# An attention-pooling recommender on one core: the order of VectorE's product and of the head's second layer

## The chip, the cores and the metric

The kernel runs on one core of a Trainium2 chip. The metric is the device time of one execution in microseconds (us); of several runs the median is taken. The profile is one more execution, taken with the hardware profiler.

## The reference

A batch of 16384 users has a history of 200 items each. Every embedding row has D = 64 numbers; the item table has some 100000 rows.

```python
it = i_emb[item]                       # [16384, 64]
h = i_emb[hist]                        # [200, 16384, 64]
itb = jnp.broadcast_to(it[None], h.shape)
feat = jnp.concatenate([h, itb, h - itb, h * itb], axis=-1)
a = dice(feat @ au_W1 + au_b1, au_alpha, axis=1)
w = a @ au_W2 + au_b2
cur = jnp.sum(w * h, axis=0)
z = jnp.concatenate([u, it, c, cur], axis=-1)
z = dice(z @ W1 + b1, alpha1, axis=0)
z = dice(z @ W2 + b2, alpha2, axis=0)
return z @ W3 + b3
```

`dice` normalises over the batch axis, takes a sigmoid p of the result, and gives `x * (p + alpha * (1 - p))`. So each of the 200 history layers needs the mean and variance of its whole batch before its weights can be computed.

## The kernel before, in words

The batch is cut into ND = 8 chunks of 2048 rows (128 partitions by TD = 16 rows). One **step** handles one chunk of one history layer; 200 layers by 8 chunks make 1600 steps. The first 168 layers run in a hardware loop (`tc.For_i`, seven passes) whose body is written out for 24 layers (192 steps); the remaining 32 layers and the head stand behind it. Inside each stretch the order of the instructions on every engine is the program's own (`manual_schedule`): an engine works through its queue in that order and waits where data aren't there.

At the start a table is built in DRAM that holds, beside each item row, that row already multiplied by its part of `au_W1`; a gather then fetches both halves, 512 bytes, at once. What depends on the item alone is computed once and kept in DRAM (`xi`).

`step(k)` works on several chunks at different ages:

- `fetch(k)`: POOL issues sixteen gathers (L202), each of 128 rows, into one of twelve landing buffers `land`; SP loads a piece of `xi` into `xit`.
- for chunk k-10, ScalarE: the sigmoid (L448) and the mixing with alpha (L451), into the PSUM tile `pg`.
- for chunk k-1: `turn` (L377), four transposes by VectorE from `land` into `hx`; ScalarE copies the transposed h into the PSUM tile `ph` (L454).
- for chunk k-2: `hidden`, VectorE adds `px` and the table's half (L390) and takes the batch statistics (L392).
- for chunk k-1: ScalarE puts `xit` into `px` (L458); `product` has VectorE multiply h by the item (L384, from `ph` and `itT` into `hx`), and TensorE adds the product of that with `blk_m` onto `px` (the L240 rows with `hx,blk_m`). The next step's `hidden` reads this `px`.
- once in a layer: `moments`, from the statistics to the scale and shift that the sigmoid uses.
- for chunk k-10: `weigh`, VectorE alone: a product (L398), a transpose (L400), a sum (L402), small copies and additions into the PSUM tile `ph` (L406, L409), the product with h (L414) and the addition to `cur` (L415).

After the last fetch ten more steps drain the pipeline, with the head's first layer between them. The head's second layer goes over the eight chunks: the activation `dice` (ScalarE L563, VectorE L564 and L565) of 64 of the hidden units, and once in four chunks (J = 4) of the rest of them; eight matmuls of 128 by 80 (L240, `w2a` and `w2b`) into one of four PSUM tiles in turn; ScalarE's copy out with the bias (L595); VectorE's statistics (L525). A third activation and the output layer (L604) end the kernel.

Of the kernel before, what the change touches and what calls it, by code (L numbers as in the profile page):

```python
# [10 lines left out]
AF = mybir.ActivationFunctionType  # L11
# [17 lines left out]
def din_kernel(  # L29
# [24 lines left out]
    nc = tc.nc  # L54
# [3 lines left out]
    ND = NT // TD  # L58
    V = i_emb.shape[0]
    A = au_W1.shape[1]  # L60
    Z1, Z2, ZO = W1.shape[1], W2.shape[1], W3.shape[1]
# [9 lines left out]
    def quarter(e, g, n=S):  # L71

        return slice((2 * e + g) * S, (2 * e + g) * S + n)
# [24 lines left out]
    for e in range(2):  # L98
        rows = au_W1.rearrange("(g d) a -> d g a", d=D)[e * S : (e + 1) * S]
        for g in range(2):  # L100
            r = quarter(e, g)
            nc.sync.dma_start(au_w[r], rows)
            for q, (a0, n) in enumerate(parts):
                c, a = quarter(q, g, n), slice(a0, a0 + n)
# [3 lines left out]
    for g in range(2):  # L108
        for q, (a0, n) in enumerate(parts):
            r, a = quarter(q, g, n), slice(a0, a0 + n)  # L110
# [18 lines left out]
    px, pz = (psum.tile([P, CD], F32, name=n) for n in ("px", "pz"))  # L129
    ph = psum.tile([P, CD], F32, name="ph")  # L130
    pg = psum.tile([P, CD], F32, name="pg")
# [9 lines left out]
    J = P // (2 * ZB)  # L141
    w1a = const.tile([P, 4, P], F32, name="w1a")
    w1b = const.tile([P, 4, P + 2 * ZB * (J - 1)], F32, name="w1b")
    w2a = const.tile([P, 2 * Z2], F32, name="w2a")
    w2b = const.tile([P, J, 2 * Z2], F32, name="w2b")
    w3 = const.tile([2 * Z2, (2 * ND - 1) * 2 * ZO], F32, name="w3")

    za, zb, z2 = (
        [const.tile([n, 1], F32, name=f"{m}{i}") for i in ("b", "al", "1al")]
        for m, n in (("za", P), ("zb", P), ("z2", 2 * Z2))  # L150
    )
# [83 lines left out]
    def layer(dst, pairs, n=CH, onto=False):  # L235

        for i in range(2):
            cols = slice(i * CH, i * CH + n)
            for j, (lhsT, rhs) in enumerate(pairs):
                nc.tensor.matmul(  # L240
                    dst[:, cols], lhsT, rhs[:, cols],
                    start=(j == 0 and not onto), stop=(j == len(pairs) - 1),
                    skip_group_check=onto,
                )
# [90 lines left out]
    with ExitStack() as main:  # L335
# [24 lines left out]
        def by_row(t):  # L360
            return t.rearrange("p (n d) -> p n d", d=D)

        def x_of(k):
            return land[k % LAND][:, :, D:]
# [16 lines left out]
        def product(k):  # L381

            hm = hx[k % 2][:, 0]
            nc.vector.tensor_mul(hm, ph, itT[:, k % ND])  # L384
            layer(px, [(blk_m, hm)], onto=True)
# [7 lines left out]
                    stats[l % 2][:, 2 * c + i, :], x_of(k)[:, ts(i, TD // 2)]  # L393
                )

        def weigh(k):

            nc.vector.tensor_mul(by_row(pg), by_row(pg), x_of(k))  # L398
            yT = hx[k % 2][:, 0]
            nc.vector.transpose(yT, pg)  # L400
            r = small.tile([P, 2, TD], F32, tag="r", name="r")
            nc.vector.tensor_reduce(  # L402
                r, yT.rearrange("p (i n u) -> p i n u", i=2, u=S), mybir.AxisListType.X, ALU.add
            )
            r1 = small.tile([D, 2, TD], F32, tag="r1", name="r1")
            nc.vector.tensor_copy(r1, r[D:])  # L406
            w = ph[:, :TD]
            for i in range(2):
                nc.vector.scalar_tensor_tensor(  # L409
                    w[ts(i, D)], r[:D, i], au_bias2[:D], r1[:, i], ALU.add, ALU.add  # L410
                )
            c = k % ND
            rows = land[k % LAND][:, :, :D]
            nc.vector.tensor_mul(by_row(pg), rows, w.unsqueeze(2).to_broadcast([P, TD, D]))  # L414
            nc.vector.tensor_add(cur[:, ts(c, TD)], by_row(pg), cur[:, ts(c, TD)])  # L415
# [22 lines left out]
        def step(k, last=None):  # L438


            def has(j):
                return last is None or j <= last

            if has(k):
                fetch(k)
            if has(k - 10):
                i = (k - 10) // ND % 2
                nc.scalar.activation(  # L448
                    by_row(pg), x_of(k - 10), AF.Sigmoid, bias=shifts[i], scale=rstds[i]
                )  # L450
                nc.scalar.activation(pg, pg, AF.Identity, bias=au_al, scale=au_1al)  # L451
            if has(k - 1):
                turn(k - 1)
                nc.scalar.copy(ph, hx[(k - 1) % 2][:, 0])  # L454
            if has(k - 2):
                hidden(k - 2)
            if has(k - 1):
                nc.scalar.copy(px, xit[(k - 1) % XI])  # L458
                product(k - 1)
            if has(k - 2) and (k - 2) % ND == ND - 1:  # L460
                moments((k - 2) // ND)
            if has(k - 10):
                weigh(k - 10)

        def fetch_ids(k, l0, n):
            l, c = divmod(k, ND)
# [40 lines left out]
        def home(i):  # L507
            t = land[(K + i // 2) % LAND].rearrange("p (s n) d -> p s (n d)", s=2)
            return t[:, i % 2]
# [6 lines left out]
        def rest_of(c):  # L516
            return home(homes[ND + c // J])
# [5 lines left out]
        def row_sums(i, n, m, t):  # L523
            for h in range(2):
                nc.vector.bn_stats(zstats[i][:, 2 * m + h, :], t[:n, ts(h, CH)])  # L525
# [18 lines left out]
        def row_factors(i, unit, n):  # L544

            mean_mat = mean_of[unit]
            mv = small.tile([P, 2], F32, tag=f"zmv{i}", name="zmv")[:n]
            nc.vector.bn_aggr(mv, zstats[i].rearrange("p c s -> p (c s)"))
            mean = ph[:n, i * 8 : i * 8 + 1]
            nc.tensor.matmul(mean, mean_mat, mv[:, 0:1], start=True, stop=True)  # L550
            dev = small.tile([P, 1], F32, tag=f"zdev{i}", name="zdev")[:n]
            nc.vector.tensor_sub(dev, mv[:, 0:1], mean)
            nc.vector.scalar_tensor_tensor(dev, dev, dev, mv[:, 1:2], ALU.mult, ALU.add)
            var = ph[:n, i * 8 + 4 : i * 8 + 5]
            nc.tensor.matmul(var, mean_mat, dev, start=True, stop=True)  # L555
            rstd = small.tile([P, 1], F32, tag=f"zrstd{i}", name="zrstd")[:n]
            shift = small.tile([P, 1], F32, tag=f"zshift{i}", name="zshift")[:n]
            return scale_and_shift(mean, var, n, rstd, shift)
# [8 lines left out]
        with tc.manual_schedule():  # L567
            work = base_of_layer1()
            for k in range(K):
                fetch_ids(k, L - rest_l, rest_l)  # L570
                step(k, last=K - 1)
                next(work, None)
            load_base(0, 1)
            for k in range(K, K + 10):
                step(k, last=K - 1)
                if k < K + 4:
                    load_base(*((2, 3), (ND, ND + 1), (4, 5), (6, 7))[k - K])
                c = k - K - 2
                if c >= 1:
                    keep1(c - 1)  # L580
                if c >= 0:
                    layer1(c)
            keep1(ND - 1)

            spare = [home(i) for i in range(18, 24)]
            fa, fb = row_factors(0, ZA, P), row_factors(1, ZB, P)
            for c in range(ND):
                if c % J == 0:
                    dice(rest_of(c), rest_of(c), spare[4 + c // J], fb, zb)
                a = spare[c % 4]  # L590
                dice(a, z_of(c), a, fa, za)
                po = (px, pz, pg, ph)[c % 4]
                layer(po[: 2 * Z2], [(w2a, a), (w2b[:, c % J], rest_of(c))])
                t = home(10 + c)[: 2 * Z2]
                nc.scalar.activation(t, po[: 2 * Z2], AF.Identity, bias=z2[0])  # L595
                row_sums(2, 2 * Z2, c, t)
            f2 = row_factors(2, Z2, 2 * Z2)
            n = ND * 2 * ZO
            for c in range(ND):
                a = spare[c % 4]  # L600
                dice(a, home(10 + c)[: 2 * Z2], a, f2, z2)
                at = (ND - 1 - c) * 2 * ZO
                for i in range(2):
                    nc.tensor.matmul(  # L604
                        px[:n, ts(i, CH)], w3[:, at : at + n], a[: 2 * Z2, ts(i, CH)],
                        start=(c == 0), stop=(c == ND - 1),
                    )

            rT, res = spare[4][:S], spare[5][:S]
            nc.vector.transpose(rT, px[:S])  # L610
            rT = rT.rearrange("t (i n c g o) -> t i g c n o", i=2, n=TD, c=ND, g=2)
            for i in range(2):
                for g in range(2):
                    nc.vector.tensor_add(
                        res[:, ts(2 * i + g, NT * ZO)].rearrange("t (c n o) -> t c n o", c=ND, n=TD),
                        rT[:, i, g],
                        bias3.unsqueeze(1).unsqueeze(1).to_broadcast([S, ND, TD, ZO]),
                    )
            nc.sync.dma_start(
                out.rearrange("(q t n) o -> t q (n o)", t=S, n=NT),  # L620
                res.rearrange("t (q m) -> t q m", q=4),
            )
# [30 lines left out]
```

## Time and profile before

| what | value |
|---|---|
| time, median of 3 runs | 36757.6 us (36756.6 to 36763.1) |
| profiled execution, its own time | 32783.1 us |
| its span, first to last instruction | 32780.9 us |
| POOL: busy, and the gathers L202 in it | 24515.6 us; 25600 of 943 ns |
| VectorE (DVE): busy | 25567.4 us |
| ScalarE (ACT), TensorE (PE): busy | 7755.2 us, 6366.6 us |
| drain and first layer of the head (32515 to 32650) | 135 us |
| second layer of the head (32650 to 32740) | 90 us |
| output layer (32740 to the end) | 41 us |

The profiled execution is shorter than the runs shown; durations below are from it. In a line of a group the columns are: line and engine, operation, output and inputs, shapes, count, then busy time in us, the mean of one in ns, and the engine's idle time just before with what ended it. "Issue" is idle time in which the engine waited for nothing that the profile shows. In a timeline they are: start and length in us, engine, line, operation, and in brackets the idle time before and what released it.

### The profile page before, as it was taken

The page shows a single profiled execution, that of the slowest core. Times are in us where ns is not written, and L with a number is a line of the kernel's source. Part 1 is how long each engine was busy: PE and PEld are TensorE (multiplying, and loading weights), DVE is VectorE, ACT ScalarE, POOL GpSimd, SP SyncE. Part 2 cuts the span into 40 slices and gives each one's busy share as a digit, 9 for nine tenths or more (in the row PEclk, how much of TensorE's full clock was granted, in tenths as well). Part 3 has the DMA queues.
Part 4 walks back from the last instruction along what each step waited for, and adds up shares of the span by engine and source line. Part 5 has one row for each costly group of instructions (what it writes and reads, how often), then busy time and mean ns, then how long its engine had stood idle before and what let it go on. Part 6 is the DMA issues. An engine that isn't in the chain of part 4 may idle for free. (4 is left out here: it accounts for less than half of the span.)

```text
span 32780.9 us, 100656 instructions
## 1 busy us (share of the span) xinstructions
PE 6366.6 (19%) x7006; PEld 2038.0 (6%) x7006; DVE 25567.4 (78%) x28797; ACT 7755.2 (24%) x7105; POOL 24515.6 (75%) x25991
## 2 busy tenths in 40 slices
PE   3111111111111111111111111111111112221112
PEld 0000000000000000000000000000000000000000
DVE  7777777777777777777777777777777777777777
ACT  1222222222222222222222222222222222222222
POOL 7777777777777777777777777777777777777775
PEclk5555555555555555555555555555555555555555
DMA  5222222222222222222222222222222223332222
GB/s 157 80 79 79 79 79 79 79 79 79 79 80 80 79 78 79 79 79 80 79 79 79 79 79 78 79 79 80 78 79 79 79 79 85 88 90 81 79 79 60
DMA packets 1214773, 2667.86 MB, mean 81 GB/s; under 512 B 551244, under 2 KB 577388, under 8 KB 1207916
## 3 DMA queue, kind: packets, MB, share of 16 engines
q0 software_dynamic: 831488, 1691.97, 19.6%
q1 hardware_dynamic: 372012, 906.09, 9.1%
q10 hardware_dynamic: 10560, 63.79, 0.5%
q14 instruction: 692, 5.67, 0.1%
q8 instruction: 21, 0.34, 0.0%
HBM read 2590.90 MB, written 69.16 MB: 81 GB/s over the span
## 5 line engine op out<-in xcount | busy, mean ns | idle before, releaser
L202 POOL DMA_INDIRECT land<-table,idx x25600 | 24152.2, 943 | 7872.6 <-issue 7703.8
L377 DVE STREAM_TRANSPOSE hx<-land 64x1024 f32<-64x1024 f32 x6404 | 7938.2, 1240 | 6360.3 <-DMA land<-table,idx 6218.5
L240 PE MATMUL px<-hx,blk_m 128*128 128x512 f32 x6408 | 5927.6, 1080 | 26007.0 <-DVE hx L384 25941.1
L448 ACT ACTIVATE pg<-land,sh,rs 128x1024 f32<-128x1024 f32 x1610 | 1943.8, 1207 | 12980.0 <-DVE cur L415 11593.3
L454 ACT COPY ph<-hx 128x1024 f32<-128x1024 f32 x1601 | 1627.6, 1017 | 10365.2 <-DVE hx L377 10362.2
L240 PEld LDWEIGHTS px<-hx,blk_m 128*128 128x128 f32 x6408 | 1880.1, 324 | 30022.8 <-issue 29846.4
L392 DVE BATCH_NORM_STATS2 st<-land 128x6 f32<-128x512 f32 x3204 | 2060.9, 685 | 55.0
L400 DVE STREAM_TRANSPOSE hx<-pg 128x1024 f32<-128x1024 f32 x1610 | 2011.7, 1250 | 55.2
L414 DVE TENSOR_TENSOR pg<-land,ph 128x1024 f32<-128x1024 f32 x1610 | 1977.8, 1228 | 55.0
L415 DVE TENSOR_TENSOR cur<-pg,cur 128x1024 f32<-128x1024 f32 x1610 | 1970.5, 1224 | 55.6
L402 DVE TENSOR_REDUCE r<-hx 128x32 f32<-128x1024 f32 x1610 | 1964.0, 1220 | 55.3
L390 DVE TENSOR_TENSOR land<-px,hx 128x1024 f32<-128x1024 f32 x1602 | 1961.6, 1224 | 49.5
L398 DVE TENSOR_TENSOR pg<-pg,land 128x1024 f32<-128x1024 f32 x1610 | 1968.8, 1223 | 2.7 <-ACT pg L451 2.5
L384 DVE TENSOR_TENSOR hx<-ph,itT 128x1024 f32<-128x1024 f32 x1601 | 1932.0, 1207 | 0.0
L451 ACT ACTIVATE pg<-pg,au_al,au_1al 128x1024 f32<-128x1024 f32 x1610 | 1895.0, 1177 | 54.3
L458 ACT COPY px<-xit 128x1024 f32<-128x1024 f32 x1601 | 1627.2, 1016 | 383.3 <-DVE land L390 381.1
L409 DVE SCALAR_TENSOR_TENSOR ph<-r,au_bias,r 64x16 f32<-64x16 f32 x3220 | 771.3, 240 | 114.8
L406 DVE COPY r<-r 64x32 f32<-64x32 f32 x1610 | 337.2, 209 | 55.0
L448 ACT ACT_TABLE_LOAD x209 | 268.1, 1283 | 452.6 <-DVE w1a L177 314.6
L249 ACT ACT_TABLE_LOAD x203 | 260.4, 1283 | 6.7 <-PE ph L555 3.2
L249 ACT ACTIVATE std<-var,eps 128x1 f32<-128x1 f32 x201 | 59.2, 295 | 475.2 <-DVE var L435 475.2
L425 DVE COPY other<-mv 32x2 f32<-32x2 f32 x804 | 155.6, 194 | 15.1
(122 smaller groups left out, 1885.8 us busy)
## 6 DMA issues: line engine op xcount, KB each, us to landing
xit<-xi SPq DMA_DIRECT2D x1601, 512.0 KB
land<-table,idx POOLq DMA_INDIRECT x25600
table<-tab ACTq DMA_DIRECT2D x48, 1024.0 KB
tab<-in_L_rec_i_emb SPq DMA_DIRECT2D x48, 512.0 KB
zt<-ucT SPq DMA_DIRECT2D x32, 512.0 KB
idx<-in_r_hist SPq DMA_DIRECT2D x200, 64.0 KB
ucT<-t ACTq DMA_DIRECT2D x16, 512.0 KB
zbase<-zt SPq DMA_DIRECT2D x10, 512.0 KB
```

The costliest lines, as they stand in the source:

```text
L202: nc.gpsimd.indirect_dma_start(out=dst[:, n, :], out_offset=None, in_=rows, in_offset=bass.IndirectOffsetOnAxis(ap=ids[:, n : n + 1], axis=0),
L240: nc.tensor.matmul(dst[:, cols], lhsT, rhs[:, cols], start=(j == 0 and not onto), stop=(j == len(pairs) - 1), skip_group_check=onto,)
L377: nc.vector.transpose(dst.rearrange("p s (n t) -> p n s t", t=S), rows[ts(i, D), :, :, e])
L384: nc.vector.tensor_mul(hm, ph, itT[:, k % ND])
L390: nc.vector.tensor_add(x_of(k), by_row(px), by_row(hx[k % 2][:, 1]))
L392: nc.vector.bn_stats(stats[l % 2][:, 2 * c + i, :], x_of(k)[:, ts(i, TD // 2)])
L398: nc.vector.tensor_mul(by_row(pg), by_row(pg), x_of(k))
L400: nc.vector.transpose(yT, pg)
L402: nc.vector.tensor_reduce(r, yT.rearrange("p (i n u) -> p i n u", i=2, u=S), mybir.AxisListType.X, ALU.add)
L414: nc.vector.tensor_mul(by_row(pg), rows, w.unsqueeze(2).to_broadcast([P, TD, D]))
L415: nc.vector.tensor_add(cur[:, ts(c, TD)], by_row(pg), cur[:, ts(c, TD)])
L448: nc.scalar.activation(by_row(pg), x_of(k - 10), AF.Sigmoid, bias=shifts[i], scale=rstds[i])
```

## The change

Two edits of order. `weigh` is cut in two: its first half, now `weights` (L398, L400, L402), runs on VectorE ahead of `product` (L384 and its matmuls), and its second half stays behind product and moments. In the head's second layer the activation and the matmuls of chunk c (`activated`) are written ahead of the copy out and the statistics of chunk c-2 (`keep2`), in place of each chunk's copy out directly behind its matmuls. No instruction is added or removed.

```diff
-        def weigh(k):
+        def weights(k):
 
             nc.vector.tensor_mul(by_row(pg), by_row(pg), x_of(k))
             yT = hx[k % 2][:, 0]
@@
                 r, yT.rearrange("p (i n u) -> p i n u", i=2, u=S), mybir.AxisListType.X, ALU.add
             )
+            return r
+
+        def weigh(k, r):
+
             r1 = small.tile([D, 2, TD], F32, tag="r1", name="r1")
             nc.vector.tensor_copy(r1, r[D:])
@@
             if has(k - 1):
                 nc.scalar.copy(px, xit[(k - 1) % XI])
+            if has(k - 10):
+                r = weights(k - 10)
+            if has(k - 1):
                 product(k - 1)
             if has(k - 2) and (k - 2) % ND == ND - 1:
                 moments((k - 2) // ND)
             if has(k - 10):
-                weigh(k - 10)
+                weigh(k - 10, r)
@@
-            for c in range(ND):
+            def activated(c):
                 if c % J == 0:
                     dice(rest_of(c), rest_of(c), spare[4 + c // J], fb, zb)
                 a = spare[c % 4]
                 dice(a, z_of(c), a, fa, za)
-                po = (px, pz, pg, ph)[c % 4]
-                layer(po[: 2 * Z2], [(w2a, a), (w2b[:, c % J], rest_of(c))])
+                layer(
+                    (px, pz, pg, ph)[c % 4][: 2 * Z2], [(w2a, a), (w2b[:, c % J], rest_of(c))]
+                )
+
+            def keep2(c):
                 t = home(10 + c)[: 2 * Z2]
-                nc.scalar.activation(t, po[: 2 * Z2], AF.Identity, bias=z2[0])
+                nc.scalar.activation(
+                    t, (px, pz, pg, ph)[c % 4][: 2 * Z2], AF.Identity, bias=z2[0]
+                )
                 row_sums(2, 2 * Z2, c, t)
+
+            for c in range(ND + 2):
+                if c < ND:
+                    activated(c)
+                if c >= 2:
+                    keep2(c - 2)
```

## The prediction

> **What bounds the kernel now.** I read the page first, then the list of waits, then the timeline of one step in mid-run, and at last the timeline of the head. Of the page, these lines carry most (busy time and share of the span; then a group's count, its busy time, the mean in ns, and the idle time before it with what ended it):
>
> ```profile
> PE 6366.6 (19%) x7006; PEld 2038.0 (6%) x7006; DVE 25567.4 (78%) x28797; ACT 7755.2 (24%) x7105; POOL 24515.6 (75%) x25991
> ...
> L202 POOL DMA_INDIRECT land<-table,idx x25600 | 24152.2, 943 | 7872.6 <-issue 7703.8
> L377 DVE STREAM_TRANSPOSE hx<-land 64x1024 f32<-64x1024 f32 x6404 | 7938.2, 1240 | 6360.3 <-DMA land<-table,idx 6218.5
> ```
>
> VectorE is the busier engine, and yet it isn't the bound. POOL's idle time before the gathers is almost all "issue": it waited for nothing, and 24152 + 7873 = 32025 us is 98% of the span. VectorE's one large wait is for the gathers to land: 6218 us, 3.9 us in each of the 1600 steps. The timeline shows the same in one step (start, length, engine, line):
>
> ```profile
> 16025.28 1.22 DVE L398 TENSOR_TENSOR pg<-pg,land 128x1024 f32<-128x1024 f32 x1
> 16025.29 0.94 POOL L202 DMA_INDIRECT land<-table,idx  x1 [0.31 <-issue]
> ...
> 16025.51 3.75 PE L240 MATMUL px<-hx,blk_m 128*128 128x512 f32 x4 [16.17 <-DVE hx L384]
> ...
> 16036.68 5.00 DVE L377 STREAM_TRANSPOSE hx<-land 64x1024 f32<-64x1024 f32 x4 [4.36 <-DMA land<-table,idx]
> ```
>
> A gather starts every 1.248 us (0.943 and 0.305 of issue), whatever VectorE is doing; sixteen make 19.97 us, and the step is 20.0 us. VectorE is done with its step at 16032.3 and then waits 4.36 us. So **POOL's gathers set the 32 ms of the loop**; what moves inside VectorE's step has 4.3 us of room.
>
> The head, the last 0.27 ms, has no gathers. In its second layer each chunk runs alone:
>
> ```profile
> 32661.12 1.11 ACT L595 ACTIVATE land<-px,z2b 80x1024 f32<-80x1024 f32 x1 [8.98 <-PE px L240]
> 32662.13 1.23 ACT L563 ACTIVATE land<-land,zshift,zrstd 128x1024 f32<-128x1024 f32 x1
> 32662.26 1.28 DVE L525 BATCH_NORM_STATS2 zst<-land 80x6 f32<-80x512 f32 x2 [7.17 <-ACT land L595]
> 32663.46 0.79 DVE L564 TENSOR_SCALAR land<-land,za1al,zaal 128x1024 f32<-128x1024 f32 x1
> 32664.29 1.22 DVE L565 TENSOR_TENSOR land<-land,land 128x1024 f32<-128x1024 f32 x1
> ...
> 32665.57 1.99 PE L240 MATMUL pz<-land,w2a 128*80 128x512 f32 x2 [4.49 <-DVE land L565]
> ...
> 32671.45 1.11 ACT L595 ACTIVATE land<-pz,z2b 80x1024 f32<-80x1024 f32 x1 [8.09 <-PE pz L240]
> ```
>
> ScalarE evacuates chunk c (L595), only then takes the sigmoid of c+1 (L563), VectorE finishes the activation, and only then TensorE starts. One chunk costs 10.33 us (32661.12 to 32671.45), of which TensorE works 5.9.
>
> **What the Trainium skill says.** (1) "SBUF — State Buffer", Who interferes with whom: a VectorE instruction with at most one SBUF input, outside the two-port modes, does not contend with GpSimd, while an fp32 copy inside SBUF can take the shared ports and hold up the writing of descriptors. The moved product L384 reads ph (PSUM) and itT, one SBUF input; the gather's 943 ns shows no trace of any of VectorE's instructions. (2) "PSUM — Partial Sum Buffer", Engine vs sequencer instructions: the queues of ScalarE and VectorE are strict FIFO. The trace agrees: L563 of the next chunk starts 1.01 us after L595 each time, never ahead of it. (3) "TensorE: Matmul & The Clock Gate", What's actually happening: the array runs at half clock until it has been busy for some 3.4 us. The trace agrees in this stage: matmuls start 0.85 us apart, after about 4.5 us of work 0.43 apart. But it does not always hold: the output layer L604 (80 rows by 32 columns) keeps 0.85 us for all of its 27.5 us.
>
> **The product moved (L384 behind L398, L400, L402).** Nothing is added or taken away in a step, no DMA among it; SP's and POOL's queues issue what they did, in the same order and past nothing new.
> - VectorE's own sum. From start to next start I read L392 to L384 0.59 us, L384 to L398 1.12, L398 to L400 1.26, L400 to L402 1.28, L402 to L406 1.25. In the new order the reduction is followed by an instruction that doesn't need its result, and so is the product: 0.59 + 1.26 + 1.28 + 1.12 + 1.12 instead of 0.59 + 1.12 + 1.26 + 1.28 + 1.25, that is 0.13 us less. It lies under the 4.3 us of waiting for the gather: worth 0.
> - What L398 now waits for: L451 of ScalarE, which ended at 16014.9 for a VectorE step that starts at 16016.7. Met.
> - What is later: TensorE's product, by 1.26 + 1.28 + 1.12 = 3.7 us. It would run from 16029.2 to 16033; who waits for it is L390 of the next step, at about 16041.7. 8.7 us of room are left. If the landing wait were gone, 4.4 us would be left.
> - The moments stay behind the product and move with it; their sqrt sits on ScalarE behind the copies, and the next sigmoid waits for L415 in either order. Worth 0.
> - The drain after the last gather (some 135 us) has one step where cover is short: the last product ends at about 32534.7, and L390, which started at 32533.8, waits some 0.9 us. Cost 1 us, once.
> - Loop ends (six between the seven passes): at the one I read, TensorE would end near 8173.1, and POOL's last gather at 8175.2 still comes last. Worth 0.
>
> **The second layer two chunks ahead.** L563 of c+1 and c+2 go ahead of L595 of c, so TensorE has two chunks queued. From the end of chunk c: 1.01 (L595) + 1.16 (L563) + 0.1 + 0.83 (L564) + 1.23 (L565) give the next operand after 4.4 us, against two chunks of 8 x 0.43 = 3.44 us, 6.9 us, that TensorE still has. TensorE becomes the bound: five matmuls at 0.85 and 59 at 0.43 make 29.6 us. VectorE's sum is as long: 8 x (1.20 + 0.83 + 1.15) + 2 x 1.98 = 29.4. Before, from the first matmul at 32655.15 to the last L595 at 32736.35 it took 81.2 us; after, 29.6 + 0.2 to reach the last L595. **Gain 51 us.** Its lower end is TensorE at half clock throughout, 64 x 0.85 = 54.6 us: gain 26. More than 53 isn't to be had, as VectorE's 29.4 remains.
>
> **Sum.** The profiled execution took 32783.1 us (span 32780.9); 32783 - 51 + 1 gives 32733. The median of the runs shown, 36757.6, stands 3974 us above it, 2.48 us for each of 1600 steps or 153 ns for each of 25984 gathers; no view says where it lies. If POOL's gathers are longer there, VectorE has more room still and the loop's part stays 0. I carry the difference over: 36757.6 - 50 = **36707**. A measurement of this kernel can tell about 0.2%, 74 us, from no change, so that counts as no change.
>
> **The rivals.**
> - *Cold TensorE.* L604's 27.5 us without a faster clock speak for it, the 0.43 us spacing inside each chunk of this very layer against. 36757.6 - 26 + 1 = 36733: no change too.
> - *VectorE is the pace of the timed runs.* For: 2.48 us per step are unexplained, and VectorE holds the most busy time. Then 0.13 us a step comes free: 1600 x 0.13 = 210 us, and with the head 36757.6 - 210 - 50 = 36498. Against: its step is 15.7 us of work, and 22.5 us would need it 40% slower than in the trace, with no wait to blame.
> - *The gather pays for the new order.* L406 is an fp32 copy inside SBUF, just of the kind that the skill says can hold up descriptors, and VectorE's phase against POOL's is fixed, since it starts on a landing. The product ahead of it puts L406 1.0 us later in a gather's 1.25 us. If a copy costs its gather up to its own 0.21 us and the 0.115 that the SBUF page (A bandwidth-pool intuition that's wrong) measured behind it, the loop grows by up to 1600 x 0.32 = 520 us; half of that gives 36757.6 + 260 - 50 = 36968, slower. It decides from 0.08 us per step on ((74 + 50) / 1600). For: the same unexplained 2.48 us. Against: in the trace the gathers around L406 are spaced like all others. The same shift could take such a cost away, which would look like the rival before.
>
> The edit not taking place is no rival: both are plain program order on in-order engines.
>
> **How the numbers follow.** No change: 0.72, mostly at 36707, own range 36700 to 36735. Faster by over 0.2%: 0.13 (VectorE as the pace, or a collision removed). Slower by over 0.2%: 0.15 (a collision added). To hold eight in ten the range takes in a loop that moves by some 0.07 us a step to either side, about a quarter of each outer case: 36600 to 36830.
>
> **What would show it.** L202 still at 943 ns and about 7700 us of "issue"; L377's wait for the landing 6200 to 6450 us; L384's matmuls 3.7 us later in the step, L390 without a wait. In the head, L595's waits gone from some 67 us to under 25, the second layer's matmuls in one row of about 30 us, mostly 0.43 us apart, and a span of 32732. Wrong if L202's spacing moves by 5 ns or more, if VectorE waits at L390 or L398 in mid-run, or if the second layer stays over 45 us.

## The result, and the profile after

| | before | after |
|---|---|---|
| median of 12 runs each | 36756.8 us (36749.1 to 36764.0) | 36766.0 us (36757.6 to 36773.3) |
| ratio | | 1.0002, 95% interval 0.9993 to 1.0011 |
| span of the profiled execution | 32780.9 us | 36760.7 us |

No change, as forecast, though 59 us above the forecast's 36707. The two spans can't be set against each other: the kernel before takes about 32785 us on some chips and about 36760 us on others. Its profile is from a chip of the first kind; the timed runs and the profile after are from the second kind. So each result below says how long before took on the same chip.

The page of after, in the rows that were shown of before (busy time and share of the span; a group's count, busy time, mean in ns, idle time before it and what ended it):

```profile
span 36760.7 us, 100656 instructions
...
PE 6368.2 (17%) x7006; PEld 2037.9 (6%) x7006; DVE 25445.5 (69%) x28797; ACT 7755.0 (21%) x7105; POOL 24516.5 (67%) x25991
...
L202 POOL DMA_INDIRECT land<-table,idx x25600 | 24153.1, 943 | 11825.8 <-issue 11629.5
```

A gather takes 943 ns as before. What grew is POOL's idle time: 11826 instead of 7873 us, 3953 us more, nearly all of the 3980 us by which this span is longer. The groups of VectorE, from the trace of after, show the other side of it:

```profile
L377 DVE STREAM_TRANSPOSE hx<-land 64x1024 f32<-64x1024 f32 x6404 | 7920.8, 1237 | 2071.6 <-issue 1973.1 <-DMA land<-table,idx 47.9 <-PEq L505 11.0
...
L418 DVE TENSOR_TENSOR pg<-land,ph 128x1024 f32<-128x1024 f32 x1610 | 1978.4, 1229 | 1190.7 <-issue 1158.6 <-DVE ph L413 16.3
...
L413 DVE SCALAR_TENSOR_TENSOR ph<-r,au_bias,r 64x16 f32<-64x16 f32 x3220 | 775.5, 241 | 3084.0 <-issue 2883.1 <-DVE r L410 117.1 <-DVE ph L413 52.2
L410 DVE COPY r<-r 64x32 f32<-64x32 f32 x1610 | 370.7, 230 | 1194.5 <-issue 976.6 <-DVE hx L384 205.1
```

VectorE waits for landings 48 us in all, where before's profile had 6218. In its place stand thousands of us of "issue": nothing to wait for, the instruction merely starts late. The timeline of after, one step in mid-run (start, length, engine, line; in brackets the idle time before):

```profile
16031.95 0.21 DVE L410 COPY r<-r 64x32 f32<-64x32 f32 x1 [1.12 <-issue]
...
16033.36 0.24 DVE L413 SCALAR_TENSOR_TENSOR ph<-r,au_bias,r 64x16 f32<-64x16 f32 x1 [1.19 <-issue]
...
16034.77 0.24 DVE L413 SCALAR_TENSOR_TENSOR ph<-r,au_bias,r 64x16 f32<-64x16 f32 x1 [1.18 <-issue]
16036.17 1.23 DVE L418 TENSOR_TENSOR pg<-land,ph 128x1024 f32<-128x1024 f32 x1 [1.16 <-issue]
16037.43 1.22 DVE L419 TENSOR_TENSOR cur<-pg,cur 128x1024 f32<-128x1024 f32 x1
16038.13 0.94 POOL L202 DMA_INDIRECT land<-table,idx  x1 [2.73 <-issue]
```

Instructions of 0.24 us start 1.41 us apart, though each has what it needs. L418, the last reader of the landing buffer, is late; and POOL, which refills that buffer, stands still for 2.73 us. The profile calls POOL's idle time "issue" too, but here it hides a wait: of POOL's 757 stops of more than 1 us between 1 and 32 ms, 736 end 0.74 us after an L418.

The delay isn't spread evenly. Counted from the first L377 of a step to that of the next, the mean step is 22.45 us: 920 of the 1600 steps last 21.5 to 23.2 us, and 371 last 15.56. The 200 steps with the moments, one in each layer, take 36.5 us on average, the other 1400 take 20.45, late ones and ones that catch up together. So of 3927 us above 20 us a step, 3298 lie in the steps with the moments. One of them, from the same trace:

```profile
16100.56 0.16 DVE L429 COPY other<-mv 32x2 f32<-32x2 f32 x1 [2.73 <-issue]
16101.95 0.16 DVE L429 COPY other<-mv 32x2 f32<-32x2 f32 x1 [1.24 <-issue]
...
16115.25 0.18 DVE L410 COPY r<-r 64x32 f32<-64x32 f32 x1 [2.61 <-issue]
...
16118.20 0.94 POOL L202 DMA_INDIRECT land<-table,idx  x1 [16.26 <-issue]
16118.64 4.99 DVE L377 STREAM_TRANSPOSE hx<-land 64x1024 f32<-64x1024 f32 x4
```

The row of short instructions comes late, L418 with it, and POOL stops for 16 us. The steps of 15.56 us come almost all in groups of four behind such a stop; in none of the 371 does POOL stop for more than 1 us.

So on such a chip VectorE, in getting its instructions, sets the pace, and not POOL. The experiments were to settle two things: whether the prediction's steps hold where POOL is the pace, and what takes its place where it isn't.

### The profile page after: what moved, and what is told of

Read it like the earlier page. It is cut to its first block, busy times and chain, and to the rows that moved or that the text cites. A ratio compares the mean times of both kernels' runs of the same rounds, so it can differ in the third digit from the quotient of the medians.

```text
span 36760.7 us, 100656 instructions
## 1 busy us (share of the span) xinstructions
PE 6368.2 (17%) x7006; PEld 2037.9 (6%) x7006; DVE 25445.5 (69%) x28797; ACT 7755.0 (21%) x7105; POOL 24516.5 (67%) x25991
## 5 line engine op out<-in xcount | busy, mean ns | idle before, releaser
L202 POOL DMA_INDIRECT land<-table,idx x25600 | 24153.1, 943 | 11825.8 <-issue 11629.5
L377 DVE STREAM_TRANSPOSE hx<-land 64x1024 f32<-64x1024 f32 x6404 | 7920.8, 1237 | 2071.6 <-issue 1973.1
L413 DVE SCALAR_TENSOR_TENSOR ph<-r,au_bias,r 64x16 f32<-64x16 f32 x3220 | 775.5, 241 | 3084.0 <-issue 2883.1
L418 DVE TENSOR_TENSOR pg<-land,ph 128x1024 f32<-128x1024 f32 x1610 | 1978.4, 1229 | 1190.7 <-issue 1158.6
L402 DVE TENSOR_REDUCE r<-hx 128x32 f32<-128x1024 f32 x1610 | 1964.1, 1220 | 584.2 <-issue 342.4
L400 DVE STREAM_TRANSPOSE hx<-pg 128x1024 f32<-128x1024 f32 x1610 | 2012.8, 1250 | 233.1 <-DVE pg L398 133.3
L390 DVE TENSOR_TENSOR land<-px,hx 128x1024 f32<-128x1024 f32 x1602 | 1962.1, 1225 | 69.7 <-issue 21.2
L398 DVE TENSOR_TENSOR pg<-pg,land 128x1024 f32<-128x1024 f32 x1610 | 1957.3, 1216 | 2.7 <-ACT pg L455 2.5
L384 DVE TENSOR_TENSOR hx<-ph,itT 128x1024 f32<-128x1024 f32 x1601 | 1945.2, 1215 | 0.0
L410 DVE COPY r<-r 64x32 f32<-64x32 f32 x1610 | 370.7, 230 | 1194.5 <-issue 976.6
```

Of the source, the lines that this page charges most:

```text
L202: nc.gpsimd.indirect_dma_start(out=dst[:, n, :], out_offset=None, in_=rows, in_offset=bass.IndirectOffsetOnAxis(ap=ids[:, n : n + 1], axis=0),
L377: nc.vector.transpose(dst.rearrange("p s (n t) -> p n s t", t=S), rows[ts(i, D), :, :, e])
L390: nc.vector.tensor_add(x_of(k), by_row(px), by_row(hx[k % 2][:, 1]))
L402: nc.vector.tensor_reduce(r, yT.rearrange("p (i n u) -> p i n u", i=2, u=S), mybir.AxisListType.X, ALU.add)
```

## The experiments

### Before again

The kernel before, unaltered, profiled once more.

> The kernel before, profiled once more. Theory A (VectorE gets its instructions late: in the profile of after its starts fall on a grid of 0.70 us and 16 working instructions take 22.4 us a step): this profile has a span near 36750 us, VectorE idle on issue before the short instructions L406 and L409, POOL waiting 2 to 3 us in a step for VectorE, gathers still 943 ns. Then the profile of before on record, 32781 us, was the odd one. Theory B (the timed runs have slower gathers, and profiles are faster): span near 32780 us again, VectorE waiting for landings.

Measured: 32785.96 us, span 32783.7. L202 943 to 944 ns with 7726 us of "issue", L377 with 6226 us of landing wait: the profile that the prediction was made from, once more. The median of 41 timed runs of the same kernel on that chip is 32785.5 us, so the 3974 us aren't an effect of profiling: here timed runs and profile agree. Theory B had the span right, but not its reason.

### The head alone

```diff
+            def activated(c):
...
+            for c in range(ND + 2):
+                if c < ND:
+                    activated(c)
+                if c >= 2:
+                    keep2(c - 2)
```

> Only the head's second layer is changed. Both theories: the second layer in one row of 30 us, 51 us less, so 36706 us. If the change's +9 us comes from the head, this run shows it.

Measured: 32735.07 against 32785.48 us, ratio 0.9985 (0.9978 to 0.9991), 50.4 us less.

### The product alone

```diff
+            if has(k - 10):
+                r = weights(k - 10)
+            if has(k - 1):
                 product(k - 1)
...
-                weigh(k - 10)
+                weigh(k - 10, r)
```

> Only the product is moved. Theory A: the order changes which instruction comes late, the count stays, so the loop stays at 22.4 us a step give or take some 0.04: between 36757 and 36820 us, and the latter if the head's 51 us were given back here. Theory B: 36757 us, no change.

Measured: 32786.55 against 32785.48 us, ratio 1.0 (0.9992 to 1.0009). The page of this kernel:

```profile
L202 POOL DMA_INDIRECT land<-table,idx x25600 | 24153.8, 944 | 7872.7 <-issue 7717.3
L377 DVE STREAM_TRANSPOSE hx<-land 64x1024 f32<-64x1024 f32 x6404 | 7938.3, 1240 | 6370.8 <-DMA land<-table,idx 6229.3
...
L390 DVE TENSOR_TENSOR land<-px,hx 128x1024 f32<-128x1024 f32 x1602 | 1961.7, 1225 | 50.2 <-PE px L240 0.7
```

POOL's 7873 us of idle time and VectorE's landing wait are those of before. The list of waits has L390 waiting for TensorE once, 0.7 us: the short cover in the drain.

### The copy on ScalarE

```diff
-            nc.vector.tensor_copy(r1, r[D:])
+            nc.scalar.copy(r1, r[D:])
```

> Before, with the copy L406 (0.2 us on VectorE) done by ScalarE. Theory A: one instruction less in VectorE's queue, worth 1.0 to 1.4 us a step, less what VectorE waits for ScalarE: 34500 to 35200 us. Theory B (POOL's gathers are the pace): VectorE has room, no change, 36757 us.

Measured: 32786.26 against 32785.48 us, ratio 1.0 (0.9992 to 1.0009); L202 943 ns as ever. Where POOL is the pace, the copy inside SBUF costs the gathers nothing that shows, and the rival that built on it has no ground there.

### The whole change where before takes 32787 us

> The kernel after, whole. On a chip where before takes 32785 us both parts add up as in the two half edits: 32785 - 50 + 1 = 32736 us. On a chip where before takes 36757 us, the head's 51 us are there too (second layer 30 us), and the loop gives them back: 36766 us again.

Measured: 32735.89 against 32786.88 us, ratio 0.9984 (0.9978 to 0.9991), 51 us less. Its page, and below it the timeline of TensorE and ScalarE in the head's second layer (L605 is L595 of before):

```profile
span 32731.8 us, 100656 instructions
...
L202 POOL DMA_INDIRECT land<-table,idx x25600 | 24153.1, 943 | 7872.6 <-issue 7732.4
L377 DVE STREAM_TRANSPOSE hx<-land 64x1024 f32<-64x1024 f32 x6404 | 7936.4, 1239 | 6380.2 <-DMA land<-table,idx 6238.4
```

```profile
32656.81 2.00 PE L240 MATMUL px<-land,w2a 128*80 128x512 f32 x2 [6.99 <-DVE land L572]
32658.60 1.91 PE L240 MATMUL px<-land,w2b 128*80 128x512 f32 x2
32660.31 1.76 PE L240 MATMUL px<-land,w2a 128*80 128x512 f32 x2
32661.91 1.02 PE L240 MATMUL px<-land,w2b 128*80 128x512 f32 x2
32662.77 1.02 PE L240 MATMUL pz<-land,w2a 128*80 128x512 f32 x2
32662.97 1.11 ACT L605 ACTIVATE land<-px,z2b 80x1024 f32<-80x1024 f32 x1 [6.90 <-PE px L240]
...
32666.40 1.11 ACT L605 ACTIVATE land<-pz,z2b 80x1024 f32<-80x1024 f32 x1 [1.19 <-PE pz L240]
```

TensorE goes from chunk to chunk without a break, at two matmuls in 0.86 us after the first five or six; the copies out follow 3.43 us apart, where before they were 10.33.

### Eight more instructions of VectorE

```diff
+        tiny = [ring.tile([P, 1], F32, name=f"tiny{i}") for i in range(8)]
...
                 weigh(k - 10)
+                for t in tiny:
+                    nc.vector.memset(t, 0.0)
```

> Before, with eight more VectorE instructions at the end of each step, memsets of one number per partition, some 0.1 us each, read by nobody. Work added: 0.6 to 1 us a step, under the 4.3 us of waiting. Theory A (VectorE's instructions are supplied at a limited rate): on a 36757 us chip each costs 1.0 to 1.4 us, 8 to 11 us a step, 49500 to 55000 us; on a 32785 us chip the supply has to keep up with 30 instructions in 20 us, and if its limit is near what the step uses now (22.4 in 20 us) the time rises there too. Theory B (POOL alone): no change on either.

Measured: 32787.6 against 32786.88 us, ratio 1.0. The timeline of this kernel:

```profile
20017.30 1.22 DVE L415 TENSOR_TENSOR cur<-pg,cur 128x1024 f32<-128x1024 f32 x1
20018.47 0.17 DVE L467 MEMSET tiny<- 128x1 f32 x8
```

All eight go in one row of 0.17 us. Where before takes 32787 us, 26 VectorE instructions a step come without delay.

### The sum on TensorE, and that with the head

```diff
-            nc.vector.tensor_copy(r1, r[D:])
...
-                nc.vector.scalar_tensor_tensor(
-                    w[ts(i, D)], r[:D, i], au_bias2[:D], r1[:, i], ALU.add, ALU.add
-                )
+                nc.tensor.matmul(w, sel[:, i], r[:, i], start=(i == 0), stop=False)
+            nc.tensor.matmul(w, bias_mat, ones, start=False, stop=True)
```

> Before, with L406 and both L409 taken from VectorE and made three small matmuls with a selection matrix, so three instructions less in its step. Theory A, on a 36757 us chip: 3 x 1.0 to 1.4 us less, which brings VectorE to POOL's 20 us a step: 32800 to 33700 us. On a 32785 us chip no change, since POOL is the pace there. Theory B: no change on either, 36757 us where before takes that.

> Before, with the three small VectorE instructions (L406, both L409) made matmuls and the head's second layer two chunks ahead. On a chip where before takes 36757 us, theory A: three instructions less in VectorE's queue bring its step from 22.4 us to 18.2 to 19.5, under POOL's 20, so 32740 to 33700 us. Theory B: 36706 us. On a chip where before takes 32785 us both: 32795 - 50 = 32745 us.

Measured: the first 32795.01 against 32786.88 us, ratio 1.0002; the second 32753.6 against 32796.9 us on another chip, ratio 0.9987 (0.998 to 0.9994). Three short VectorE instructions less in a step shorten nothing while POOL is the pace: the waits of the first kernel show what became of them.

```profile
DVE hx L393 <- DMA land<-table,idx: 5472.4, 1587, 6.6
DVE pg L427 <- PE ph L424: 2093.7, 1609, 2.2
```

VectorE waits 2094 us for TensorE's sum, and so less for the landing (5472 us). With the head's edit the 43 us gained are that edit's 51 less the 8 that the matmuls cost. As a way out where VectorE's instructions come late, these two ran on chips of the other kind, so whether fewer short instructions help there isn't known. The same holds of the product alone and of the copy on ScalarE.

### Half of the gathers, without and with the product moved

```diff
-        for k in range(-10, 0):
+        for k in range(-12, 0):
             nc.vector.memset(land[k % LAND], 0.0)
...
-            gather(land[k % LAND], idx[l % IDX][:, ts(c, TD)], table)
+            gather(land[k % LAND], idx[l % IDX][:, c * TD : c * TD + TD // 2], table)
```

> Before, with eight gathers in a step in place of sixteen: half of the history rows are left out (the landing buffers keep old rows there). POOL then needs 10 us a step, and VectorE has to be the pace. If VectorE gets its instructions as fast as it can work, 15.6 us a step: about 25.5 ms. If they come at a limited rate of their own, as in the profile of after, 22.4 us a step and 36.5 ms with half the gathers too; if it is the gathers' traffic that holds them up, between 15.6 and 22.4.

> Half the gathers (half of the history rows left out, as in the run before), and the product moved: VectorE is the pace, so its own sum is measured. By the term of the prediction, 0.13 us a step less: 26270 - 210 = 26060 us. By the starts in the profile of after, where the reduction to the product is 1.14 us but the product to the copy L410 is 1.25 and not 1.12, nothing is won: 26270 us. On a chip where before takes 36757 us: near 22.4 us a step or 36.5 ms if VectorE's instructions come late with half the gathers too.

Measured: 26270.7 us in the old order (before on that chip 32796.9, ratio 0.801, 0.7994 to 0.8026), 26366.0 us in the new (before on that chip 36777.5, ratio 0.7169, 0.7157 to 0.7181). The pages of both, old order first:

```profile
span 26268.4 us, 87824 instructions
...
PE 6377.5 (24%) x7006; PEld 2042.1 (8%) x7006; DVE 25344.9 (96%) x28799; ACT 7755.7 (30%) x7105; POOL 12444.6 (47%) x13191
```

```profile
span 26363.1 us, 87824 instructions
...
PE 6388.2 (24%) x7006; PEld 2044.3 (8%) x7006; DVE 25347.5 (96%) x28799; ACT 7756.0 (29%) x7105; POOL 12436.2 (47%) x13191
...
L413 DVE SCALAR_TENSOR_TENSOR ph<-r,au_bias,r 64x16 f32<-64x16 f32 x3220 | 771.1, 239 | 114.8
```

VectorE is the bound in both, 96% busy. Two readings. First, the new order isn't shorter on VectorE: a step takes 15.92 or 15.93 us on average in both (from the starts of L377), so the prediction's 0.13 us isn't there. Most steps last the forecast 15.6 us (15.56); the one with the moments lasts 18.4, which the forecast of 25.5 ms left out: some 570 us of the 770 that it missed. Second, the chip on which before takes 36777 us ran the loop at the full speed of VectorE as soon as POOL gathered half of the time: L413's 2883 us of "issue", which after's trace has, are gone.

The 95 us between the two spans lie ahead of the loop: the first L377 starts at 621.9 us instead of 524.5. There POOL issues the gathers of users, items and categories one behind the other, 1.25 us apart, and the list of VectorE's waits up to 620 us has late starts in the second trace that the first doesn't have:

```profile
DVE tab L231 <- issue: 67.2, 54, 15.9
DVE rT L223 <- issue: 42.2, 49, 1.5
```

So in one and the same execution VectorE is late under dense gathers and not under half as many. The late start isn't a slower VectorE; it comes with the gathers. Whether POOL's work of issuing them counts or their traffic, these runs don't part.

### Thirty-two more instructions, without and with the product moved

The edit is that of the eight, with 32; the second kernel has the product in its new place too.

> Before, with 32 more VectorE instructions in each step, memsets of one number per partition that nobody reads. Work: 32 x some 0.07 us = 2.2 us, still under the 4.3 us of waiting. If a chip supplies VectorE's instructions at a limit anywhere above 0.37 us each (20 us over 54), the time rises: at 0.5 us to 27 us a step, 43 ms. If not, 32787 us as with eight. On a chip where before takes 36757 us: 54 us a step and more, over 85 ms, if each instruction costs 1.0 us there.

> The product in its new place (the head as before), and 32 one-element memsets of VectorE at the end of each step; nothing is left out. It depends on the chip it runs on, and each case is written down. On a chip where before takes about 32785 us: theory A (late issue of VectorE's instructions belongs to some chips only) says the 32 memsets run in one row, 8 ns apart, some 0.4 us a step, hidden under the 3.9 us of waiting for the gathers; 32786 to 32800 us, L377 still waiting for the landing, some 5500 us. Theory B (VectorE's instructions are handed out at a limited pace on every chip while gathers run, only slower on some) says that a row of memsets breaks off after some 22 and goes on at a fixed spacing of some tenths of a us, and the time rises above 32900. On a chip where before takes about 36760 us: theory A and B say the same as was seen in the row with 32 memsets in the old order, a burst of about 22 memsets and then one each 0.70 us, 42000 to 42300 us; a difference of more than 150 us from 42153 would mean that the order of product and weighting matters for the late issue.

Measured: 42152.9 us in the old order (before 36777.5 on that chip, ratio 1.1461, 1.1439 to 1.1484), 43478.4 us in the new (before 36762.4, ratio 1.1825, 1.1805 to 1.1845). Both met chips on which before takes about 36770 us. The pages differ most in POOL's idle time, old order first:

```profile
L202 POOL DMA_INDIRECT land<-table,idx x25600 | 24151.3, 943 | 17198.2 <-issue 17115.1
```

```profile
L202 POOL DMA_INDIRECT land<-table,idx x25600 | 24163.8, 944 | 18476.8 <-issue 18345.8
```

The timeline of the new order with 32 shows what "late" means. First a step that begins after POOL had stood still for 11.3 us, then one under gathers:

```profile
20006.26 0.94 POOL L202 DMA_INDIRECT land<-table,idx  x1 [11.31 <-issue]
20006.73 0.58 DVE L474 MEMSET tiny<- 128x1 f32 x32
```

```profile
20026.10 0.35 DVE L474 MEMSET tiny<- 128x1 f32 x12
20027.10 0.06 DVE L474 MEMSET tiny<- 128x1 f32 x1 [0.65 <-issue]
20028.49 0.06 DVE L474 MEMSET tiny<- 128x1 f32 x1 [1.33 <-issue]
20029.19 0.06 DVE L474 MEMSET tiny<- 128x1 f32 x1 [0.65 <-issue]
20029.91 0.06 DVE L474 MEMSET tiny<- 128x1 f32 x1 [0.65 <-issue]
```

With POOL idle just before, 32 instructions of 0.06 us run in one row of 0.58 us. Under gathers twelve do in the step shown, and the others come one by one, most of them 0.70 us apart or a multiple of it. Over the whole trace the first row ends after 20 to 23 memsets in 718 of 1610 steps (717 in the old order); all 32 go in one row in 158 (735 in the old order). It reads as a store of instructions that are ready, which runs empty, and is filled slowly while POOL gathers and quickly when it doesn't. The 0.70 us is the grid and not the mean pace: the late memsets start 1.0 us apart on average (0.96 in the old order). After's step holds 16 working VectorE instructions and some five that only handle semaphores; 21 at 1.0 us are 21 us, an estimate from these two traces, near the 21.5 to 23.2 us of most steps.

The mean price is far lower: 5375 us for 32 x 1600 instructions is 0.105 us each, not 1.0 to 1.4 us as my first theory of a fixed price per instruction had it. The likely reason is that a delay stops POOL, and each stop refills the store.

The two orders differ by 1325 us (0.83 us a step), far over the 150 us that were written down as the mark; before differs by only 15 us between the two chips. So where VectorE's instructions come late, the place of the product matters, and the new one is the dearer, as far as one chip for each order can say: that both chips hold VectorE's instructions back alike isn't shown.

## Why the prediction was right, and where it wasn't

**The verdict and the steps hold where POOL is the pace.** There the sum, 32783 - 51 + 1 = 32733 with a span of 32732, met 32735.9 us and a span of 32731.8.
- *The second layer.* Forecast 29.8 us from first matmul to last copy out; measured 32687.00 - 32656.81 = 30.2 (before 81.2). Five matmuls at half speed were forecast, some six came. The ceiling of 53 us was a slip: 81.2 - 29.4 is 51.8. The copies' waits fell from 67 to 16 us (under 25 was forecast). The cold rival is out: here the faster clock came.
- *The product.* Its matmuls start 3.68 us later in a step (forecast 3.7); L390 waits once, 0.7 us (forecast 0.9); L202's time and spacing and L377's landing wait stand (6238 us, forecast 6200 to 6450). Net +1.1 us, forecast +1.
- *VectorE's own sum* was wrong. The 0.13 us came from giving two pairs the 1.12 us of L384 to L398, because their second instruction doesn't need the first one's result. In the new order L402 to L384 is 1.14 us and L384 to L410 1.25, not 1.12 and 1.12: the step's own work remains 15.56 us either way. Nothing rested on it but the rival, whose 210 us fell with it.

**The step that failed is the last one of the sum**: carrying the 3974 us of the timed runs over as a POOL with longer gathers and a VectorE with more room. On those chips a gather is still 943 ns, and 1.25 us from the next wherever POOL doesn't stop. But two of the prediction's own signs fail there: L202 has 11630 us of "issue", not 7700, and L377 waits 48 us for landings, not 6200 to 6450. After's span is 4029 us longer than the span of the same kernel on the other kind of chip, of which 97 us lie ahead of the first L377 and 3933 between the first and the last, where POOL stops 2.5 us a step on average, over half of it in the steps with the moments, for a buffer that a late VectorE frees.

So the rival "VectorE is the pace of the timed runs" had the right engine. Its argument against, that VectorE would need 40% longer "with no wait to blame", overlooked that a trace can show late instructions as idle time without a wait. It had the sign wrong: the new order doesn't gain 0.13 us a step, and with 32 more instructions it loses.

That 36766 us lies within 36600 to 36830 is in part luck. The sum missed by 59 us, more than the 51 us that it priced, and it was the allowance of 0.07 us a step to either side, given without a cause, that took the miss in; the loop's move was some 0.04. "No change" itself was safer: 51 us are less than 0.2%, given back or not.

**Where the 51 us went.** In after's trace the head is as fast as in the kernel above: its second layer's matmuls run from 36686.2 to 36716.2 us, two in 0.86. With the head's 51 us the median should have been 36706; it was 36766. Some 60 us, 0.04 us a step, were given back ahead of the head: a ratio of 0.9986 lies outside of the measured 0.9993 to 1.0011, if the head of before takes as long on such a chip as in its profile. The product's place is the only other edit, so it is the likely cost, but shown in size only with 32 more instructions (0.83 us a step), and there on two chips; the product alone wasn't run on such a chip.

**Still open.** (1) Why the order matters there. In the new order the once-a-layer moments, a row of short instructions, stand directly ahead of L410 and L413, also short, with no long one between for the store to fill, and that step is the dear one in after's trace; but no trace of before on such a chip stands beside it, and with 32 more all steps of a layer but one grow, not just that one (31.8 to 33.0 us), so this isn't the whole cause. (2) What hands VectorE its instructions late, and why on some chips only; each chip was used at one time only, so it can also be a state that a chip stays in for a while. The volume of instructions isn't it: "Vector Engine (DVE) Microarchitecture Reference", Instruction fetch and dispatch, in the Trainium skill gives 64 bytes for each, and the profile agrees, with 1095 instead of 692 packets of 8 KB for 51520 more (403 x 8192 / 51520 = 64), but that queue has 0.1% of the span. Nor is a packet slower: its median is 0.46 us in after's trace and on the other kind of chip. (3) Whether the gathers' issue or their traffic is to blame. (4) Whether the other chips have the same limit at a higher pace: 26 instructions a step passed there, 50 weren't tried.

## What to carry to other kernels

Before carrying a profile's slack over to a median that stands elsewhere, explain the distance between them: 3974 us unexplained meant another engine at the bound, and the 4.3 us of cover in each step were not there in the runs that count. An engine can be slow without being busy and without a wait: look for short instructions with "issue" before them at even spacing, and count instructions, not only their durations. And "issue" can hide a wait, as POOL's did: compare the end of a stop with what ended just before it. A mean step hides where the time goes: here one step in eight held 3298 of 3927 us. Stages without gathers, like the head here, were priced well from one profile, and their gain can still drown in a loop of 36 ms.

## What was not expected of the hardware

- On some chips short VectorE instructions came 0.70 us apart or a multiple of it under POOL's gathers, 1.0 us on average, once a row of mostly 20 to 23 had gone; right after a stop of POOL, 32 ran in 0.58 us. The mean step of after is 22.45 us there instead of 20.0, and 36.5 us where the row of short instructions of the moments falls.
- After a stop of some 16 us VectorE ran four steps at its full speed of 15.56 us, though POOL gathered all through them.
- With half of the gathers, the same kind of chip ran the loop at 15.92 us a step, like the other kind.
- The gather's 943 ns, and its spacing of 1.25 us where POOL didn't stop, were the same on both kinds of chip.
